# Causal attention over 1024 tokens: queries kept in natural token order, score pieces of five visits dealt anew, projections moved between visits

## The chip, the cores and the metric

The kernel runs on one NeuronCore of one Trainium2 chip. The metric is the device time of one execution in microseconds. It is given as the median of several executions. A profile is one further execution, recorded instruction by instruction.

## What is computed

`x` holds 32 images of 256 channels by 1024 tokens (32 x 32), in float32. Each image goes through a group norm (32 groups of 8 channels), a projection to queries, keys and values, causal attention with 8 heads of 32 channels in which a token sees only earlier tokens, and a residual sum. Cut to what matters, for one image:

```python
xn = _gn(x)                                     # 32 groups of 8 channels, eps 1e-5
q = einsum('oc,bcs->bos', q_w, xn) + q_b
k, v = halves of einsum('oc,bcs->bos', kv_w, xn) + kv_b
scores = einsum('bhqd,bhkd->bhqk', q, k) / sqrt(32)
scores = where(tril(ones, -1) == 0, -10000.0, scores)
attn = softmax(scores); attn = where(mask == 0, 0.0, attn)
x = x + einsum('bhqk,bhkd->bhqd', attn, v)
```

The mask leaves out the diagonal, so that the first token sees nothing.

## The kernel before, in words

**Tiling.** Channels lie on the 128 partitions in two groups `g` of four heads each. Tokens are cut into eight blocks of 128. Scores are kept transposed, keys on partitions and queries along the row, so that the exponentials can be fed to the product with the values without a transpose. No maximum is subtracted; a slow path (`shifted`) would redo everything if a sum left its range, and it isn't run here. In odd blocks the tokens of the normed input `xn` are stored backwards (`norm_apply`, L260). In the kernel before, queries, keys and values all inherit that order, and `finish` (L626) turns the result back.

**Visits.** The work of one image on one group is cut into five visits (the table `VISITS`, L676), so an image has ten, called 0 to 9 here: 0 to 4 for the first group, 5 to 9 for the second. A visit makes, for each of four heads, the scores of one key block against 512 queries ("L", tiles `sT`, one tile of two PSUM banks for each pair of heads), and against up to 384 more queries short pieces that share one tile of three banks (`tri`). ScalarE then makes three exponentials from it (L449 and L452): `e` for the first pair of heads, `e` for the second, `eh` for the short pieces. GpSimd zeroes what the mask hides (`mask`, L399). A string in `VISITS` gives the order in which TensorE gets the pieces: `2L` is the long row of head 2, `3s2` the piece "s" of head 3 in bank 2, and `W` is a wait of TensorE on its own earlier products, since two heads must not write one bank at once. The head pair that is named in the fourth entry goes into the first `sT` tile.

**The loop.** The main loop (L867) puts into each engine's queue, in this order: the scores of visit i; the first part of the products with the values of visit i-1 (`values(..., 0)`, tile `acc`); the projections that the table `PROJECT` (L765) puts at this visit; the second part of the products; the sums of keys on VectorE (`add_keys`); and what is set "after" the visit, among it the halves of the norm for the next image (`norm_apply`, placed by `PREPARE`, L766). Queues run in order, so this order is that of every engine.

**Projections.** An image has twelve units of projection: query or key, group, half of the tokens (tiles `pp`, eight units), and two token blocks of values each (tiles `ppv`, four units). Two of the ten visits take two units, the others one. `PROJECT` counts visits from the start of the image that the unit belongs to, so that -4 is visit 6 of the image before. Each unit needs a PSUM bank. `room` (L136) gives half of a tile from the pool of the `sT` tiles; that pool has two tiles in all, so they are passed round between the two pairs of heads and the projections. `lone` (L133) gives the one bank of the pool that the accumulators `acc` of the values use as well. ScalarE copies each unit out (L287, L306).

```python
ps_s = tc.alloc_tile_pool(name="ps_s", bufs=2, space=PSUM)
ps_t = tc.alloc_tile_pool(name="ps_t", bufs=1, space=PSUM)
ps_o = tc.alloc_tile_pool(name="ps_o", bufs=1, space=PSUM)
...
def lone(name):
    return ps_o.tile([P, HALF], F32, tag="acc", name=name)
```

`norm_*`, `fold`, `stack`, `sum_folded`, `invert` and `spread_inverses` make the statistics of the norm and the denominators with VectorE, GpSimd and DMAs; the change leaves them where they are.

Of the kernel before, what the change touches and what calls it, by code (L numbers as in the profile page):

```python
# [17 lines left out]
P = 128  # L18
HD = 32
# [14 lines left out]
def tile_norm_attention_residual(  # L34
# [69 lines left out]
    def unshifted():  # L104
# [68 lines left out]
        def product(out, lhsT, rhs, start=True, stop=True, more=1):  # L173


            for c in range(P // HD):
                part, n = slice(HD * c, HD * (c + 1)), more if c == 0 else 1
                width = rhs.shape[-1] // n
                for k in range(n):
                    cols = slice(k * width, (k + 1) * width)  # L180
                    nc.tensor.matmul(  # L181
                        out[part, cols], lhsT=lhsT[:, part], rhs=rhs[:, cols], start=start, stop=stop, skip_group_check=True
                    )
# [91 lines left out]
        def project_qk(b, g, n, hf, bank=room):  # L275

            key = ("qk"[n], b, g)
            if hf == 0:
                live[key] = qkpool.tile([P, S], F32, tag="qk"[n], name=f"{'qk'[n]}_{b}_{g}")
            cols = slice(hf * HALF, (hf + 1) * HALF)  # L280
            pp = bank(f"pp_{b}_{g}_{n}_{hf}")
            for cc in range(NG):
                product(
                    pp, wT[:, cc, n * C + g * P : n * C + (g + 1) * P], live["xn", b, hf][:, cc, :],
                    start=cc == 0, stop=cc == NG - 1, more=2 if (g, n, cc) == (0, 0, NG - 1) else 1,
                )
            nc.scalar.activation(  # L287
                live[key][:, cols], pp, AF.Identity, bias=qk_bias[:, n, g : g + 1], scale=(SCALE, 1.0)[n],
            )
            if (g, n, hf) == (1, 1, 0):  # L290
                nc.scalar.sem_inc(copied, 1)

        def project_v(b, n, bank=room):
# [5 lines left out]
            hf, at = divmod(2 * n * P, HALF)  # L299
            for s in range(2):  # L300
                tokens = slice(at + s * P, at + (s + 1) * P)
                for cc in range(NG):
                    product(
                        pp[:, s, :], live["xn", b, hf][:, cc, tokens], wT[:, cc, 2 * C : 3 * C], start=cc == 0, stop=cc == NG - 1,
# [3 lines left out]
        def projections(b):  # L308
# [4 lines left out]
            def v(n, *bank):  # L313
# [4 lines left out]
                qk(0, 0, 0, *early), qk(1, 0, 0), qk(0, 0, 1, *early), v(0, *early), qk(1, 0, 1), qk(0, 1, 0, lone),  # L318
                qk(1, 1, 0), v(1), v(2), v(3), qk(0, 1, 1), qk(1, 1, 1, lone),
            ]  # L320

        def both(label, kb, first, width, at=0):

            return [(label, c, at, kb, first, width) for c in (0, KEYS)]

        def row(kb, blocks, more=()):
# [3 lines left out]
                ("o", 0, 0, kb + 1, (kb + 1) * P, KEYS), ("o", KEYS, 0, kb + 1, (kb + 1) * P, P),  # L330
                ("e", 0, KEYS, kb, kb * P, blocks * P),
                ("e", KEYS, P, kb, kb * P + KEYS, blocks * P - KEYS),
            ] + list(more)

        def pieces(i):
# [4 lines left out]
            for j in range(4):  # L340
                for label, c, at, k, q, width in short:
                    at += j * SHORT
                    while width:
                        bank = at // HALF
                        n = min(width, (bank + 1) * HALF - at)
                        ops.setdefault((j, label, bank), []).append((j, c, bank, at, k, q, n))
                        at, q, width = at + n, q + n, width - n
                for label, a, b in (("L", 0, HALF), ("La", 0, HALFBANK), ("Lb", HALFBANK, HALF)):
                    ops[j, label, None] = [(j, c, None, a, kb, first + a, b - a) for c in (0, KEYS)]
            return ops  # L350

        def program(i):
# [4 lines left out]
            for word in VISITS[i][4].split():  # L357
# [3 lines left out]
                else:  # L361
                    j, label = int(word[0]), word[1:]
                    key = (j, label, None) if label[0] == "L" else (j, label[:-1], int(label[-1]))
# [19 lines left out]
        def score(b, g, to, op):  # L383

            j, c, _, at, kb, first, width = op
            rows = slice(HD * j, HD * (j + 1))
            return nc.tensor.matmul(  # L387
                to[c : c + KEYS, at : at + width], lhsT=live["k", b, g][rows, kb * P + c : kb * P + c + KEYS],
                rhs=live["q", b, g][rows, first : first + width], start=True, stop=True, skip_group_check=True,
            )  # L390

        def select(to, of, odd):

            nc.gpsimd.affine_select(  # L394
                out=to, in_=of, pattern=[[0, 4], [(1, -1)[odd], P]], compare_op=ALU.is_gt, fill=0.0, base=0,
                channel_multiplier=(-1, 1)[odd],
            )

        def mask(b, g, i):  # L399
# [3 lines left out]
            if i == 0:  # L403
                select(e[:, :, :P], e[:, :, :P], 0)
                nc.gpsimd.memset(e[0:1, :, 0:1], 1.0)
                select(eh[:, :, :P], eh[:, :, :P], 1)
            elif i < 4:
                square = epool.tile([P, 4, 2 * P], F32, tag="d", bufs=3, name=f"diagonal_{b}_{g}_{i}")
                live["e", b, g, "D", i] = square
                for s in range(2):  # L410
                    select(square[:, :, s * P : (s + 1) * P], eh[:, :, (1 - s) * KEYS : (3 - s) * KEYS], s)

        def scores(b, v):
# [6 lines left out]
            wide = max(at + width for _, _, at, _, _, width in short)  # L420
# [205 lines left out]
        def finish(b, n, within=slice(0, HALF), later=None, queue=nc.sync):  # L626
# [4 lines left out]
            start, count = within.start // P, (within.stop - within.start) // P  # L631

            def add(s):
                nc.vector.scalar_tensor_tensor(  # L634
                    blocks(rb, s), blocks(num, s, (start + s) % 2 == 1), v_bias_col[:, g : g + 1],
                    blocks(xt[:, g, cols], s), ALU.add, ALU.add,
                )

            def end():
                if cols.start == 0:  # L640
# [7 lines left out]
            parts = min(count, 2)  # L648
            return [lambda: nc.vector.tensor_mul(num, num, rb)] + [lambda s=s: add(s) for s in range(parts - 1)] + [  # L649
                lambda: (add(parts - 1), end())  # L650
            ]

        def end_last(b):
# [8 lines left out]
            for n, part in enumerate([in_range] + bounds):  # L662
# [12 lines left out]
        WHOLE = "1s0 2s1 3s2 0L 2L 1L 3L W 0s0 1s1 W 2s2"  # L675
        VISITS = [  # L676
            (0, 0, both("s", 1, P, 3 * P), (0, 2), WHOLE),
            (0, HALF, row(2, 2), (2, 3), "2e2 1e1 3La 0e0 0o0 3Lb 2L 1L 0L W 3e2 3o2 2e1 W 1o0 2o1 1e0"),
            (
                1, HALF, row(4, 1, both("x", 5, 6 * P, P + KEYS, P + KEYS)), (2, 3),  # L680
                "1e1 2x2 0x0 3Lb 0o0 1x1 2Lb 0e0 3La 1Lb 2La W 0Lb 3o2 1La 3x2 W 2o1 0La 2e1 1o0 3e2 1e0 2x1",
            ),
            (
                2, HALF, row(6, 2, both("x", 5, 7 * P + KEYS, KEYS, 2 * P + KEYS)), (0, 1),
                "3x2 1o0 2o1 0Lb 1e0 2e1 3e2 1Lb 3o2 0La 2Lb 1La 3Lb W 0o0 2La 0e0 3La 1e1 0x0 W 2e2 2x2 1x1",
            ),
            (3, HALF, both("s", 4, 5 * P, 3 * P), (0, 2), WHOLE),
# [7 lines left out]
                0, [(("H", 0, Q(0, 3)), 1, Q(1, 4)), (("H", 1, Q(1.5, 2.5)), 2, Q(3, 4))],  # L695
# [3 lines left out]
            (  # L699
                1, [(("L", 3, Q(0, 4)), 2, Q(0, 4)), (("H", 2, Q(1.5, 3)), 5, Q(2, 3.5))], [  # L700
                    (("H", 3, Q(2.5, 3)), 5, Q(3.5, 4)),
                    (("D", 2, Q(0, 1)), 4, Q(0, 1)), (("D", 2, Q(1, 2)), 5, Q(1, 2)),
                ],
            ),
# [359 lines left out]
```

## Time and profile before

| | |
|---|---|
| time, median of 3 runs | 1780.82 us (1780.32 to 1783.55) |
| time of the profiled execution | 1780.62 us |
| its span, first to last instruction | 1778.9 us |
| granted TensorE clock | 0.999 |
| busy: TensorE, VectorE, ScalarE, GpSimd | 99%, 92%, 82%, 48% |

The span divided by 32 images is 55.6 us for an image. In the timelines a row is: start and length in us, the engine (PE is TensorE, PEld its weight loads, ACT ScalarE, DVE VectorE, POOL GpSimd), the line, the operation, output tile <- input tiles, shapes, and how many of them were merged. A float32 product takes two records in the profile, so that the counts are twice those of the program. What stands in brackets is the idle time ahead of the row and what ended it.

### The profile page before, as it was taken

Reading aid. Unit: us, or ns where it says so; the run is one execution under the profiler, and the core shown is the slowest. Engines: PE = TensorE matmul, PEld = TensorE weight load, DVE = VectorE, ACT = ScalarE, POOL = GpSimd, SP = SyncE. Lnnn points to the kernel's source line nnn. Section 1 sums busy time; section 2 is a strip of 40 time slices with the busy share of each in tenths; the row PEclk is TensorE's granted clock in tenths of the full one; section 3 lists DMA queues with packets and bytes.
Section 4 is the critical chain, followed back from the end, with each engine's and each line's share of the span. In section 5 each row is a group of like instructions: output and inputs, shape, how many; then the busy total and the mean of one; then the engine's idle time right before and its main releaser. Section 6 shows DMA issues by size and latency. Waiting matters only on the chain.

```text
span 1778.9 us, 81945 instructions
## 1 busy us (share of the span) xinstructions
PE 1765.2 (99%) x37152; PEld 982.5 (55%) x37152; DVE 1631.3 (92%) x1859; ACT 1465.8 (82%) x1736; POOL 855.3 (48%) x935
## 2 busy tenths in 40 slices
PE   9999999999999999999999999999999999999997
PEld 5555555555555555555555555555555555555553
DVE  4689999999999999999999999999999999999987
ACT  6888888888888888888888888888888888888885
POOL 2445544544554455444454544555445455455541
PEclk9999999999999999999999999999999999999999
DMA  2566766766767767776677676666766676777663
GB/s 70 108 119 133 149 131 147 139 137 141 145 134 139 146 135 150 128 151 135 137 142 149 130 143 142 140 144 130 144 143 139 140 141 137 146 136 143 130 119 87
DMA packets 92772, 240.22 MB, mean 135 GB/s; under 512 B 26273, under 2 KB 27793, under 8 KB 76545
## 3 DMA queue, kind: packets, MB, share of 16 engines
q0 software_dynamic: 17360, 100.58, 38.5%
q1 hardware_dynamic: 74912, 134.28, 26.9%
q8 instruction: 291, 4.77, 1.1%
q14 instruction: 65, 0.52, 0.1%
q10 hardware_dynamic: 144, 0.07, 0.0%
HBM read 69.90 MB, written 34.95 MB: 59 GB/s over the span
## 4 chain that ended last, share of the span: by engine, by line
PE 97%; DVE 1%; DMA 1%; ACT 0%; issue 0%; SPq 0%; POOL 0%; DVEq 0%; ACTq 0%
PE acc L478 30%; PE pp L181 25%; PE tri L387 16%; PE sT L387 14%; PE ppv L181 12%; DMA rb<-inverses 0%; DMA x<-in_x_dram 0%; ACT e L449 0%; DVE rb L634 0%; DVE num L649 0%; ACT eh L452 0%; DMA inverses<-inv_turned 0%; DVE rb_last L634 0%; DVE e L497 0%; DVE st L197 0%
## 5 line engine op out<-in xcount | busy, mean ns | idle before, releaser
L449 ACT ACTIVATE e<-sT 128x1024 f32<-128x1024 f32 x640 | 620.8, 1022 | 232.5 <-PE sT L387 229.2
L387 PE MATMUL sT<-q,k 32*64 32x256 f32 (+1 forms) x7424 | 547.8, 461 | 0.3 <-issue 0.3
L387 PE MATMUL tri<-q,k 32*64 32x128 f32 (+4 forms) x12416 | 539.2, 297 | 1.0 <-ACT eh L452 0.9
L394 POOL TENSOR_SCALAR_AFFINE_SELECT diagonal<-eh 128x512 f32<-128x512 f32 x384 | 366.3, 993 | 300.3 <-ACT eh L452 300.3
L387 PEld LDWEIGHTS tri<-q,k 32*64 32x64 f32 x12416 | 387.1, 131 | 172.9 <-issue 79.9
L181 PE MATMUL pp<-xn,wT 128*32 128x512 f32 (+1 forms) x4224 | 477.6, 582 | 0.0
L497 DVE TENSOR_TENSOR e<-e,e 128x2048 f32<-128x2048 f32 x189 | 467.9, 2476 | 3.4
L497 DVE TENSOR_TENSOR e<-e,eh 128x1536 f32<-128x1536 f32 x378 | 420.7, 1113 | 41.4 <-PE acc L478 33.7
L452 ACT ACTIVATE eh<-tri 128x1536 f32<-128x1536 f32 (+1 forms) x320 | 453.4, 1417 | 1.1 <-PE pd L550 1.1
L524 POOL DMA_DIRECT2D e<-e x248 | 213.6, 861 | 368.4 <-DMA e<-e 282.4
L478 PE MATMUL acc<-e,v 128*32 128x512 f32 x2560 | 338.8, 600 | 1.5 <-POOL diagonal L394 1.5
L387 PEld LDWEIGHTS sT<-q,k 32*64 32x64 f32 x7424 | 302.8, 131 | 12.2 <-issue 0.6
L181 PEld LDWEIGHTS pp<-xn,wT 128*32 128x32 f32 x4224 | 140.6, 109 | 270.3 <-issue 215.7
L497 DVE TENSOR_TENSOR e<-e,diagonal 128x1024 f32<-128x1024 f32 x189 | 253.4, 1341 | 6.7
L181 PE MATMUL ppv<-wT,xn 128*32 128x256 f32 x4064 | 242.6, 379 | 0.0
L478 PE MATMUL acc<-eh,v 128*32 128x384 f32 (+3 forms) x3072 | 198.7, 346 | 0.0
L394 POOL TENSOR_SCALAR_AFFINE_SELECT e<-e 128x512 f32<-128x512 f32 x64 | 96.6, 1509 | 201.9 <-ACT e L449 201.9
L478 PEld LDWEIGHTS acc<-eh,v 128*32 128x32 f32 x3072 | 97.0, 110 | 143.1 <-issue 120.6
L181 PEld LDWEIGHTS ppv<-wT,xn 128*32 128x32 f32 x4064 | 130.9, 110 | 70.0 <-ACT q L287 0.3
L649 DVE TENSOR_TENSOR num<-num,rb 128x512 f32<-128x512 f32 x124 | 95.4, 790 | 62.4 <-DMA rb<-inverses 60.6
L273 ACT ACTIVATE xn<-x,shift,rstd 128x256 f32<-128x256 f32 x248 | 135.1, 593 | 0.4 <-POOL shift L258 0.4
L634 DVE SCALAR_TENSOR_TENSOR rb<-num,v_bias_col,x 128x256 f32<-128x256 f32 x248 | 123.7, 521 | 0.0
(94 smaller groups left out, 1226.9 us busy)
## 6 DMA issues: line engine op xcount, KB each, us to landing
e<-e POOLq DMA_DIRECT2D x124, 512.0 KB, 6.5
x<-in_x_dram SPq DMA_DIRECT2D x124, 256.0 KB, 4.3
e<-e POOLq DMA_DIRECT2D x124, 256.0 KB, 4.6
folded<-e SPq DMA_DIRECT2D x124, 256.0 KB, 4.5
rb<-inverses SPq DMA_DIRECT2D x124, 256.0 KB, 3.4
out_dram<-rb SPq DMA_DIRECT2D x124, 256.0 KB, 3.8
x<-in_x_dram SPq DMA_DIRECT2D x2, 512.0 KB, 3.7
inverses<-inv_turned SPq DMA_DIRECT2D x31, 32.0 KB
```

Of the source, the lines that this page charges most:

```text
L181: nc.tensor.matmul(out[part, cols], lhsT=lhsT[:, part], rhs=rhs[:, cols], start=start, stop=stop, skip_group_check=True)
L273: nc.scalar.activation(to, of, AF.Identity, bias=live["shift", b][:, g : g + 1], scale=rstd)
L387: return nc.tensor.matmul(to[c : c + KEYS, at : at + width], lhsT=live["k", b, g][rows, kb * P + c : kb * P + c + KEYS], rhs=live["q", b, ...
L394: nc.gpsimd.affine_select(out=to, in_=of, pattern=[[0, 4], [(1, -1)[odd], P]], compare_op=ALU.is_gt, fill=0.0, base=0, channel_multiplier= ...
L449: nc.scalar.activation(e[:, heads[a][0] : heads[a][1] + 1 : step, :], banks[a], AF.Exp)
L452: exp = nc.scalar.activation(eh[:, :, :wide], tri.rearrange("p (j q) -> p j q", q=SHORT)[:, :, :wide], AF.Exp)
L478: nc.tensor.matmul(acc[HD * j : HD * (j + 1), of], lhsT=live["v", b][:, kb, h * HD : (h + 1) * HD], rhs=e[:, j, :], start=first, stop=last ...
L497: nc.vector.tensor_add(to, to, tile_of(b, g, at))
L524: nc.gpsimd.dma_start(out=total[:rows], in_=total[rows : 2 * rows], accum_op=ALU.add)
L634: nc.vector.scalar_tensor_tensor(blocks(rb, s), blocks(num, s, (start + s) % 2 == 1), v_bias_col[:, g : g + 1], blocks(xt[:, g, cols], s), ...
L649: return [lambda: nc.vector.tensor_mul(num, num, rb)] + [lambda s=s: add(s) for s in range(parts - 1)] + [lambda: (add(parts - 1), end())]
```

## The change

**Queries in natural order.** The query projection reads the backward blocks of `xn` in reverse. For that, `project_qk` cuts each product of 512 columns, for queries and keys, into two of 2 x 128 (even blocks, odd blocks), and for queries the odd half is read backwards. The splitting of one product in `product` (`more`) goes. `finish` no longer turns anything back and makes one addition of 512 columns out of two of 256.

**Scores.** Visits 0 and 5 leave 64 x 64 pieces out that the mask hides, and use their place for pieces of the diagonal of block 4 ("z", in the first 64 columns of the long row; "y", among the short pieces). Visits 2 and 3 of each group share out the rest in another way: visit 3 now makes 320 short columns for each head in place of 384, visit 2 makes the 384 with fewer and longer products. The string of visit 0 becomes `2s2 0z 1s1 0y0 3L 0s0 2L 1z 1L 3z 2z 0L W ...`, and its first pair of heads is 2 and 3 in place of 0 and 2. The products with the values of visit 3 change from 512, 192 | 64, 128, 128 columns to 512, 384 | 128. A new tile `corner` holds the diagonal of block 4; `mask` fills it with two selects and a copy on GpSimd, and two selects of 128 columns become one of 128 and two of 64.

**Places of the projections.** `PROJECT` and `projections` change, and with them what shares a visit: visit 1 has two units of the second group, visit 6 two of the next image. `PREPARE` moves two operations of the norm from after visit 6 to after visit 5, and one from after visit 7 to after visit 6.

```diff
-        def product(out, lhsT, rhs, start=True, stop=True, more=1):
+        def product(out, lhsT, rhs, start=True, stop=True):
...
-            for cc in range(NG):
-                product(
-                    pp, wT[:, cc, n * C + g * P : n * C + (g + 1) * P], live["xn", b, hf][:, cc, :],
-                    start=cc == 0, stop=cc == NG - 1, more=2 if (g, n, cc) == (0, 0, NG - 1) else 1,
-                )
+            for s in range(2):
+                for cc in range(NG):
+                    product(
+                        blocks(pp, s), wT[:, cc, n * C + g * P : n * C + (g + 1) * P],
+                        blocks(live["xn", b, hf][:, cc, :], s, n == 0 and s == 1), start=cc == 0, stop=cc == NG - 1,
+                    )
...
-                qk(0, 0, 0, *early), qk(1, 0, 0), qk(0, 0, 1, *early), v(0, *early), qk(1, 0, 1), qk(0, 1, 0, lone),
-                qk(1, 1, 0), v(1), v(2), v(3), qk(0, 1, 1), qk(1, 1, 1, lone),
+                qk(0, 0, 0, *early), qk(1, 0, 0), qk(0, 0, 1, *early), qk(1, 0, 1), v(0, lone), v(1, *early),
+                qk(0, 1, 0), qk(1, 1, 0), qk(0, 1, 1, lone), v(2), qk(1, 1, 1), v(3),
...
             if i == 0:
-                select(e[:, :, :P], e[:, :, :P], 0)
+                corner = live["e", b, g, "C", i] = epool.tile([P, 4, P], F32, tag="c", bufs=1, name=f"corner_{b}_{g}")
+                select(corner[:, :, KEYS:], e[:, :, :KEYS], first=KEYS)
+                select(e[:, :, :P], e[:, :, :P])
                 nc.gpsimd.memset(e[0:1, :, 0:1], 1.0)
+                nc.gpsimd.tensor_copy(corner[:KEYS, :, KEYS:], eh[:KEYS, :, :KEYS])
+                select(eh[:, :, :P], eh[:, :, :P], 1)
...
             def end():
+                nc.vector.scalar_tensor_tensor(rb, num, v_bias_col[:, g : g + 1], xt[:, g, cols], ALU.add, ALU.add)
...
-            (0, 0, both("s", 1, P, 3 * P), (0, 2), WHOLE),
+                ], (2, 3), "2s2 0z 1s1 0y0 3L 0s0 2L 1z 1L 3z 2z 0L W 3s2 2s1 2y1 W 1s0 3y2 1y0",
...
-        PROJECT = (-5, -4, -2, -3, 0, 1, 1, -1, 2, 4, 3, 6)
-        PREPARE = (-13, -12, -10, -10, -9, -8, -7, -6, -4, -4, -3)
+        PROJECT = (-5, -4, -3, -2, -4, -1, 0, 1, 1, 2, 3, 4)
+        PREPARE = (-13, -12, -10, -10, -9, -8, -7, -6, -5, -4, -4)
...
-            for n, f in zip((None, None, 0, None, 0, 1, 1, 1) + PROJECT[8:], units):
+            for n, f in zip((None,) * 5 + (0,) + PROJECT[6:], units):
```

Three places of the queues follow, as the built programs have them. Names carry the group, the query/key number and the half: `pp_1_0_1` is the second group's query on the second half of the tokens, `e_0_1` the exponentials of visit 1. A semaphore named after an engine is a wait for that engine.

TensorE from the end of the scores of visit 1 to the first scores of visit 2, before the change. Here `pp_1_0_0` is the unit in the accumulators' bank (`lone`) and `pp_1_1_0` the one in a tile of the `sT` pool (`room`):

```order
L387 MATMUL tri_0_1_3844<-q_0_3373,k_0_3468 64x64
L181 MATMUL pp_1_0_0_3888<-xn_0_3250,wT 32x512 [waits Activation_49]
L181 MATMUL pp_1_0_0_3888<-xn_0_3250,wT 32x512 x7
L181 MATMUL pp_1_1_0_3899<-xn_0_3250,wT 32x512 [waits Activation_49]
L181 MATMUL pp_1_1_0_3899<-xn_0_3250,wT 32x512 x7
L478 MATMUL acc_0_0_3910<-e_0_0_3766,v_3572 32x512 [waits Activation_49,Pool_49]
L478 MATMUL acc_0_0_3910<-e_0_0_3766,v_3572 32x512 x3
```

The same place after the change; `pp_1_1_0` has the tile of the `sT` pool, and `pp_1_0_1` the accumulators' bank:

```order
L399 MATMUL tri_0_1_3920<-q_0_3438,k_0_3535 64x64 x2
L178 MATMUL pp_1_1_0_3966<-xn_0_3313,wT 32x2x128 [waits Activation_49]
L178 MATMUL pp_1_1_0_3966<-xn_0_3313,wT 32x2x128 x15
L178 MATMUL pp_1_0_1_3985<-xn_1_3488,wT 32x2x128 x16
L497 MATMUL acc_0_0_4003<-e_0_0_3822,v_3554 32x512 [waits Activation_49,Pool_49]
L497 MATMUL acc_0_0_4003<-e_0_0_3822,v_3554 32x512 x3
```

The two units have changed places: the one in the accumulators' bank now stands directly ahead of the accumulators, and the one in the `sT` pool directly behind the scores. In the program, its first product waits for the first exponential of visit 1, and the first product of `acc` for ScalarE's copy of the unit ahead of it. Visit 6 has the same order, with `pp_0_1_0` and then `ppv_0` of the next image.

TensorE from the last projection of visit 4 into the scores of visit 5, before:

```order
L181 MATMUL ppv_3_4158<-wT,xn_1_3494 32x256 x15
L478 MATMUL acc_0_1_4089<-eh_0_3_4034,v_3572 32x64 x4
L478 MATMUL acc_0_1_4089<-diagonal_0_2_3983,v_3572 32x128 [waits Pool_49]
L478 MATMUL acc_0_1_4089<-diagonal_0_2_3983,v_3572 32x128 x3
L478 MATMUL acc_0_1_4089<-diagonal_0_2_3983,v_3572 32x128 [waits Pool_49]
L478 MATMUL acc_0_1_4089<-diagonal_0_2_3983,v_3572 32x128 x3
L387 MATMUL tri_1_0_4200<-q_1_3887,k_1_3898 64x128 [waits Activation_49]
L387 MATMUL tri_1_0_4200<-q_1_3887,k_1_3898 64x128
L387 MATMUL tri_1_0_4200<-q_1_3887,k_1_3898 64x256 x2
L387 MATMUL tri_1_0_4200<-q_1_3887,k_1_3898 64x384 x2
L387 MATMUL sT_1_0_0_4198<-q_1_3887,k_1_3898 64x512 x4
L387 MATMUL sT_1_0_1_4199<-q_1_3887,k_1_3898 64x512 [waits Activation_49]
```

And after:

```order
L178 MATMUL ppv_3_4223<-wT,xn_1_3488 32x256 x15
L497 MATMUL acc_0_1_4147<-corner_0_3860,v_3554 32x128 x4
L399 MATMUL tri_1_0_4256<-q_1_3876,k_1_3965 64x128 [waits Activation_49]
L399 MATMUL tri_1_0_4256<-q_1_3876,k_1_3965 64x128
L399 MATMUL sT_1_0_1_4255<-q_1_3876,k_1_3965 64x64
L399 MATMUL tri_1_0_4256<-q_1_3876,k_1_3965 64x256 x2
L399 MATMUL tri_1_0_4256<-q_1_3876,k_1_3965 64x64
L399 MATMUL sT_1_0_0_4254<-q_1_3876,k_1_3965 64x512 [waits Activation_49]
```

The products with the values behind the projection shrink from three groups of four to one, and the second `sT` tile to be written (in both programs that is the one that waits for ScalarE's copy of `ppv_3`) now comes behind a 64-column piece of the other tile, in place of the four long rows of a whole pair of heads. Visit 9 and visit 0 of the next image have the same two rows of waits.

ScalarE from the copy of visit 5's projection to the first exponential of visit 6, before and then after:

```order
L287 ACTIVATE q_0_5968<-pp_0_0_0_5969,qk_bias 128x512 [waits PE_49,Activation_49]
L487 COPY num_0_1_5999<-acc_0_1_5819 128x512 [waits PE_49]
L449 ACTIVATE e_1_1_6011<-sT_1_1_0_6013 128x1024 [waits DMASW6_49,DMAHW6_49,DMASW5_49,PE_49]
L449 ACTIVATE e_1_1_6011<-sT_1_1_1_6014 128x1024 [waits PE_49]
L452 ACTIVATE eh_1_1_6012<-tri_1_1_6015 128x4x320 [waits DVE_49,PE_49,Pool_49]
```

```order
L285 ACTIVATE q_0_6039<-pp_0_0_0_6040,qk_bias 128x512 [waits PE_49,Activation_49]
L506 COPY num_0_1_6077<-acc_0_1_5881 128x512 [waits PE_49]
L270 ACTIVATE xn_1_6089<-x_5192,shift_5800,rstd_5695 128x2x128 [waits DMAHW7_49]
L270 ACTIVATE xn_1_6089<-x_5192,shift_5800,rstd_5695 128x2x128
L468 ACTIVATE e_1_1_6092<-sT_1_1_0_6094 128x1024 [waits DMASW6_49,DMAHW6_49,DMASW5_49,PE_49]
```

Two operations of the norm have moved in ahead of the first exponential of visit 6.

More of the change, by code (lines that the diff above doesn't have):

```diff
@@ L171, in keep_busy @@
                 nc.tensor.matmul(pt[:width, 0, :width], lhsT=ident[:, :width], rhs=ident[:, :width], start=True, stop=True)
-        def product(out, lhsT, rhs, start=True, stop=True, more=1):
+        def product(out, lhsT, rhs, start=True, stop=True):
             for c in range(P // HD):
[L177 to L182, printed above, removed]
-                    )
+                part = slice(HD * c, HD * (c + 1))
+                nc.tensor.matmul(
+                    out[part], lhsT=lhsT[:, part], rhs=rhs, start=start, stop=stop, skip_group_check=True
+                )
         def blocks(tokens, s, turned=False):
@@ L646, in end @@
                     later(send)
[L648 to L651, printed above, removed]
+            return [lambda: nc.vector.tensor_mul(num, num, rb), end]
         def end_last(b):
```

125 lines of the change are left out of this document (66 added, 59 removed).

## The prediction

> **What bounds the kernel now.** I read the page first, then the waits of TensorE, then a table by stretches, and then the timelines of TensorE and ScalarE over a few visits.
>
> ```profile
> span 1778.9 us, 81945 instructions
> PE 1765.2 (99%) x37152; PEld 982.5 (55%) x37152; DVE 1631.3 (92%) x1859; ACT 1465.8 (82%) x1736; POOL 855.3 (48%) x935
> PE 97%; DVE 1%; DMA 1%; ACT 0%; issue 0%; SPq 0%; POOL 0%; DVEq 0%; ACTq 0%
> PE acc L478 <- POOL diagonal L394: 1.5, 1, 1.5
> PE pp L181 <- ACT k L287: 0.8, 1, 0.8
> 900.00:955.40 55.40, 55.40 (x1164) 30.56 (x1160) 52.21 (x60) 46.62 (x56) 27.88 (x31) 1.00 0.72 142
> ```
>
> The chain that ends last is TensorE's for 97% of the span. Its two longest waits add up to 2.3 us of 1778.9, and over one image of 55.4 us it has no idle time at all. So TensorE's work and its waits set the time: what its stages lose or gain counts in full, and every new wait counts in full. VectorE (52.2 us of 55.4), ScalarE (46.6) and GpSimd (27.9) have room.
>
> The changed order matters in three places of each group of five visits. The profiled execution took 1780.62 us, within 0.2 us of the median 1780.82, so I add to it and leave the difference.
>
> **Wait (a), the projection behind the scores of visits 1 and 6.** The timelines of TensorE and ScalarE around a visit 1, the group of the exponentials, and the one place of the start where TensorE waits for a copy:
>
> ```profile
> 897.69 0.39 PE L387 MATMUL tri<-q,k 32*64 32x64 f32 x4
> 899.28 3.64 PE L181 MATMUL pp<-xn,wT 128*32 128x512 f32 x32
> 902.74 1.04 PE L478 MATMUL acc<-e,v 128*32 128x512 f32 x8
> 898.93 1.94 ACT L449 ACTIVATE e<-sT 128x1024 f32<-128x1024 f32 x2 [0.52 <-PE sT L387]
> 902.99 0.69 ACT L287 ACTIVATE k<-pp,qk_bias 128x512 f32<-128x512 f32 x1 [0.42 <-PE pp L181]
> L449 ACT ACTIVATE e<-sT 128x1024 f32<-128x1024 f32 x640 | 620.8, 1022 | 232.5 <-PE sT L387 229.2
> 24.56 2.76 PE L181 MATMUL pp<-xn,wT 128*32 128x512 f32 x24
> 27.38 0.69 ACT L287 ACTIVATE k<-pp,qk_bias 128x512 f32<-128x512 f32 x1 [0.79 <-PE pp L181]
> 28.12 1.93 PE L181 MATMUL pp<-wT,xn 128*32 128x256 f32 x32 [0.81 <-ACT k L287]
> ```
>
> Scores start at 897.69, the two units of projection at 899.28. The first exponential runs from 898.93 for 1.02 (row L449), to 899.95. Today the unit in the accumulators' bank goes first and needs none of it. After the change the unit in the `sT` pool goes first, and its tile is the one that this exponential reads. From the end of ScalarE's row at 28.07 to TensorE at 28.12 it took 0.05, so the unit can start at 900.00: 0.72 us of wait where there was none, at visit 1 of 32 images. Visit 6 has two operations of the norm ahead of its exponential in addition:
>
> ```profile
> 870.58 0.58 ACT L487 COPY num<-acc 128x512 f32<-128x512 f32 x1
> 871.69 1.94 ACT L449 ACTIVATE e<-sT 128x1024 f32<-128x1024 f32 x2 [0.53 <-PE sT L387]
> 913.79 1.08 ACT L273 ACTIVATE xn<-x,shift,rstd 128x256 f32<-128x256 f32 x2
> ```
>
> ScalarE was idle 0.53 us at that place, and two such operations take 1.08, so the exponential comes about 0.45 later, allowing 0.1 for the overlap of ScalarE's rows: 1.17 us at visit 6 of 31 images. Sum (a): 0.72 x 32 + 1.17 x 31 = 59.3 us.
>
> **Wait (b), the accumulators behind the projection in their own bank.** The rows at 24.56 to 28.12 above show this case once today: a projection ends at 27.32, ScalarE copies it from 27.38 to 28.07, and TensorE goes on at 28.12, idle 0.81. In the steady state today, another unit of 1.73 us lies between. After the change `acc` follows the unit directly, twice in an image. Without a wait it would start before the unit's last product ends:
>
> ```profile
> 906.34 1.91 PE L181 MATMUL ppv<-wT,xn 128*32 128x256 f32 x32
> 908.07 0.62 PE L478 MATMUL acc<-diagonal,v 128*32 128x128 f32 x16
> 911.24 1.90 PE L181 MATMUL pp<-xn,wT 128*32 128x512 f32 x16
> 912.96 1.04 PE L478 MATMUL acc<-e,v 128*32 128x512 f32 x8
> L306 ACT COPY v<-ppv 128x512 f32<-128x512 f32 x127 | 74.4, 586 | 2.4 <-PE ppv L181 1.0
> ```
>
> The next work starts 1.73 after the start of a unit that ends after 1.91, so 0.18 more is lost: 0.99 us behind a query (visit 1), and 0.88 behind values, whose copy takes 0.59 in place of 0.69 (visit 6). Sum (b): 0.99 x 32 + 0.88 x 31 = 59.0 us. Behind TensorE's waiting product stand only its own scores of the next visit; ScalarE waits for those, and has no other work that could be drawn forward.
>
> **Wait (c), the long rows of visits 0 and 5.** The second `sT` tile that is written waits for ScalarE's copy of the values projected before:
>
> ```profile
> 915.62 1.06 PE L478 MATMUL acc<-e,v 128*32 128x512 f32 x8
> 916.82 1.91 PE L181 MATMUL ppv<-wT,xn 128*32 128x256 f32 x32
> 918.55 0.29 PE L478 MATMUL acc<-eh,v 128*32 128x64 f32 x8
> 918.66 0.62 PE L478 MATMUL acc<-diagonal,v 128*32 128x128 f32 x16
> 919.21 0.56 PE L387 MATMUL tri<-q,k 32*64 32x128 f32 x6
> 919.25 0.64 PE L387 MATMUL sT<-q,k 32*64 32x512 f32 x2
> 920.90 1.06 PE L478 MATMUL acc<-e,v 128*32 128x512 f32 x8
> 922.43 1.92 PE L181 MATMUL pp<-xn,wT 128*32 128x512 f32 x18
> 917.32 1.46 ACT L452 ACTIVATE eh<-tri 128x1536 f32<-128x1536 f32 x1
> 918.80 0.58 ACT L306 COPY v<-ppv 128x512 f32<-128x512 f32 x1
> ```
>
> Today the copy is over at 919.38, and the scores start at 919.21; four long rows lie ahead of the first one that needs the tile. After the change the products ahead of the projection are 512 and 384 columns, as in the rows from 920.90 to 922.43: 1.53 in place of 1.20. The projection then starts at 917.15 and ends at 919.06; the copy lasts until 919.71, and TensorE can go on at 919.76. The products behind the projection shrink from 0.66 (918.55 to 919.21) to some 0.33 (half of the 0.55 from 918.66, and the tail), so the scores still start at 919.21. But `3L` now comes after some seven short pieces (0.05 us to issue, as six records take 0.04 to the row at 919.25), and stands from 919.26 to 919.76. Everything behind it stands too, and head 3 has nothing before it, so the stage becomes longer by the whole 0.50. Sum (c): 0.50 x 63 = 31.5 us.
>
> **What is gained.** Lengths of the scores, from their first row to the next work: visit 1 1.59 (897.69 to 899.28), visit 5 1.69 (919.21 to 920.90), and visit 3:
>
> ```profile
> 908.62 0.35 PE L387 MATMUL tri<-q,k 32*64 32x64 f32 x6
> 910.36 1.06 PE L478 MATMUL acc<-e,v 128*32 128x512 f32 x8
> ```
>
> That is 1.74, and visit 2 has the same pieces. Visit 3 becomes like visit 1 (320 short columns, much the same pieces): -0.15. Visit 2 keeps its 384 columns in 24 products in place of 43; visit 5 needs 1.69 for them in 20: about 1.70, -0.04. Visit 0 goes from 20 to 28: +0.01. Together -0.18 x 64 = -11.5 us. The products with the values keep their sum (1.53 + 0.33 against 1.20 + 0.66). Query and key units become as finely cut as the value units: 1.73 against 1.72 above, 256 units, +2.5 us. In visits 3 and 8 the second `sT` tile is reached sooner; its copy ends some 0.3 to 0.4 into the scores, about where it is wanted: 0 to 7 us, I take 3.
>
> At nothing I cost: the merged addition in `finish` and the merged sums (VectorE, below its limit); the shorter exponential of visit 3 (ScalarE, below it); GpSimd's two or three more operations for a group, which have at least the scores of the next visit as cover (without it, a wait like the 1.5 us of `acc` on `diagonal` in the waits above); the moved units' copies on ScalarE, since each visit keeps its number of units; the start and the end of the program, 2 us either way.
>
> [...]
>
> **Sum.** 59.3 + 59.0 + 31.5 - 11.5 + 2.5 + 3 = 143.8. 1780.6 + 143.8 = 1924 us.
>
> **The rivals.**
>
> 1. The waits stay hidden and the kernel gets faster. For: two units in one visit cost no wait today, and less is computed. Against: that rests on the order of the two units, which has been turned round. The time would be 1780.6 - 11.5 + 2.5 = 1771.6. It decides at 0.14 us of wait for each of the 63 groups; (b) alone is some 0.9. Chance 4%, and 1% for something within 0.2% of the time before, about what measurement of this kernel can tell.
>
> 2. Only the accumulators' wait shows in full. The order of visit 1 starts head 3 early, so that the first exponential may come sooner, and 3L may find its tile copied. (a) can't go under 0.4 us: a long row of 512 columns takes at least 0.85 (half of the 1.73 in which a unit streams 1024 such columns), and 0.85 + 1.02 + 0.1 is past 1.59. Time: 1780.6 + 0.4 x 63 + 59.0 - 9 = 1856. Chance 8%.
>
> 3. Reading backwards is slow on TensorE. No row shows it. On ScalarE odd blocks are read backwards today at no visible cost:
>
> ```profile
> L273 ACT ACTIVATE xn<-x,shift,rstd 128x256 f32<-128x256 f32 x248 | 135.1, 593 | 0.4 <-POOL shift L258 0.4
> 882.03 0.61 ACT L273 ACTIVATE xn<-x,shift,rstd 128x256 f32<-128x256 f32 x1
> ```
>
> The single one is a backward half, 0.61 against a mean of 0.59 over both kinds. If TensorE took twice as long, half of four query units of 1.73 would add 3.46 us to an image: 1924 + 111 = 2035. Below nothing isn't to be had, since the columns are the same. Chance 5%.
>
> 4. The pauses lower the clock. If the stage behind each of the four long pauses of an image (a projection of 1.73, products of 0.97) ran at half speed, it would add 2 x (1.73 + 0.97) x 31.5 = 170: 2094. Chance 2%.
>
> The forecast itself has the remaining 80%. Its own range: (a) moves by 0.25 us a time (16), (b) by 0.1 (6), (c) between 0.2 and 0.7 (-19, +13), the scores by 5, start and end by 2; about 1880 to 1965. To leave out no more than 2 in 10 it reaches down to rival 2: 1856 to 1965. Slower 0.95, faster 0.04, same 0.01.
>
> **What would show it.** In the changed profile TensorE's waits should list `pp` on ScalarE's `e` 63 times with some 0.7 to 1.2 us, `acc` on ScalarE's `q` and `v` copies 63 times with about 0.8 and 0.7 us of idle time, and `sT` on `v` 63 times with about 0.5. TensorE's busy share should fall to 93 to 95%, and scores of visit 3 should take 1.6 us. The forecast is wrong if an image's stretch shows TensorE without idle time, if query units take longer than key units, or if the granted clock falls below 1.00.

## The result, and the profile after

The changed kernel takes 1962.91 us (median of 4 runs, 1958.14 to 1966.85); before it was 1781.18 beside them. The ratio is 1.1017 (95% interval 1.099 to 1.1044): slower, by more than the 1924 forecast, and close under the upper end of the range. The profiled execution took 1963.14 us. First its page, and its chain of waits:

```profile
span 1961.4 us, 82054 instructions
PE 1831.6 (93%) x37144; PEld 1089.5 (56%) x37144; DVE 1579.3 (81%) x1668; ACT 1458.8 (74%) x1736; POOL 959.0 (49%) x1191
q8 instruction: 291, 4.77, 1.0%
PE 86%; ACT 8%; issue 3%; DMA 2%; DVE 1%; POOL 1%; ACTq 0%; SPq 0%; DVEq 0%; POOLq 0%
```

TensorE was busy for 99% and is now for 93%. ScalarE, which had no part of the chain, has 8% of it. The third line is used further down; "issue" in the last one, 3%, is time in which TensorE waited for nothing that the profile shows. TensorE's waits (total us, times, longest):

```profile
PE pp L178 <- ACT e L468: 57.2, 63, 1.1
PE acc L497 <- ACT q L285: 28.8, 32, 0.9
PE acc L497 <- ACT v L304: 24.7, 31, 0.8
PE tri L399 <- issue: 4.6, 8, 1.1
PE sT L399 <- issue: 1.4, 1, 1.4
```

The first three are waits (a) and (b), at 63 places each, as named. The last two were not foreseen. The sign that was named for (c), `sT` on `v` in this list, isn't in it: other products of TensorE are still running at that place. The list of the weight loads has it, at 62 places:

```profile
PEld sT L399 <- ACT v L304: 20.9, 62, 0.3
```

A visit 1 on TensorE, and below it on ScalarE:

```profile
1531.87 0.28 PE L399 MATMUL tri<-q,k 32*64 32x64 f32 x4
1534.43 3.66 PE L178 MATMUL pp<-xn,wT 128*32 128x256 f32 x64 [0.91 <-ACT e L468]
1538.99 1.07 PE L497 MATMUL acc<-e,v 128*32 128x512 f32 x8 [0.90 <-ACT q L285]
```

```profile
1533.36 1.94 ACT L468 ACTIVATE e<-sT 128x1024 f32<-128x1024 f32 x2 [0.77 <-PE sT L399]
1538.16 0.69 ACT L285 ACTIVATE q<-pp,qk_bias 128x512 f32<-128x512 f32 x1 [1.04 <-PE pp L178]
```

The first exponential starts 1.49 us after the scores, not 1.24, and the projection waits for it. The two units then stream 64 products, a query and a key unit alike, and `acc` stands until ScalarE has copied the second one. Visit 6 is the same with the norm's operations ahead of the exponential. In visit 0 the rows of TensorE show wait (c) as a hole between two groups of scores, and ScalarE's row shows what fills it:

```profile
1525.63 0.33 PE L399 MATMUL tri<-q,k 32*64 32x128 f32 x2
1525.77 0.53 PE L399 MATMUL tri<-q,k 32*64 32x64 f32 x5
1526.18 0.64 PE L399 MATMUL sT<-q,k 32*64 32x512 f32 x2
```

```profile
1525.55 0.59 ACT L304 COPY v<-ppv 128x512 f32<-128x512 f32 x1 [0.34 <-PE ppv L178]
```

The long row starts 0.04 behind the end of the copy (1526.14). The stages, as the mean of 27 images each, the fourth to the thirtieth (us; from the first row of a visit's scores to that of the next visit; the third column is an experiment told below):

| visit | before | changed | changed, without GpSimd's transfers |
|---|---|---|---|
| 0 | 5.70 | 6.24 | 6.24 |
| 1 | 6.02 | 8.36 | 8.12 |
| 2 | 4.90 | 4.86 | 4.86 |
| 3 | 5.31 | 5.67 | 5.29 |
| 4 | 5.29 | 5.28 | 5.28 |
| 5 | 5.73 | 6.24 | 6.24 |
| 6 | 6.03 | 8.17 | 8.13 |
| 7 | 4.90 | 4.86 | 4.86 |
| 8 | 5.34 | 5.39 | 5.40 |
| 9 | 5.29 | 5.28 | 5.28 |
| image | 54.50 | 60.34 | 59.68 |

**The stops.** In visits 1 and 3 the length varies from image to image, which no wait of the theory explains: visit 3's scores take 1.59 us in the best images and 3.72 in the worst. A visit without such a stop is called undisturbed below. One such visit 3, on TensorE:

```profile
943.51 1.15 PE L399 MATMUL sT<-q,k 32*64 32x256 f32 x11
946.03 0.58 PE L399 MATMUL sT<-q,k 32*64 32x512 f32 x1 [1.37 <-issue]
946.03 0.76 PE L399 MATMUL tri<-q,k 32*64 32x64 f32 x20
```

TensorE and its weight loads stand together. A record is an entry of the profile for a product, a weight load or one of about 80 other instructions of TensorE's queue, most of them for semaphores. Counting these from the start, gaps of 0.5 to 2.0 us in visit 3 lie behind records 22208, 29120, 31424, 33728 and 36032: each is a multiple of 256, plus 192. The page has 37144 + 37144 products and weight loads of TensorE and 291 packets of instructions, one for 255 records. And in the window from 943.6 to 944.6 us the DMA view shows one of them:

```profile
q8 instruction: 1, 0.02, 5.8%
```

TensorE goes on 1.4 us behind that packet. What stood ahead of it in the queues, on GpSimd and SyncE:

```profile
936.95 0.89 POOL L543 DMA_DIRECT2D e<-e  x1
```

```profile
937.80 5.61 SPq L655 DMA_DIRECT2D out_dram<-rb  x3
```

The first is one of GpSimd's accumulating transfers (two for each sum of the keys, 512 and 256 KB), the second the results on their way out. TensorE passed the beginning of the block before at 938.8, and the packet began only at 943.65.

### The profile page after: what moved, and what is told of

Read it like the earlier page. It is cut to its first block, busy times and chain, and to the rows that moved or that the text cites. A ratio compares the mean times of both kernels' runs of the same rounds, so it can differ in the third digit from the quotient of the medians.

```text
span 1961.4 us, 82054 instructions
## 1 busy us (share of the span) xinstructions
PE 1831.6 (93%) x37144; PEld 1089.5 (56%) x37144; DVE 1579.3 (81%) x1668; ACT 1458.8 (74%) x1736; POOL 959.0 (49%) x1191
## 3 DMA queue, kind: packets, MB, share of 16 engines
q8 instruction: 291, 4.77, 1.0%
## 4 chain that ended last, share of the span: by engine, by line
PE 86%; ACT 8%; issue 3%; DMA 2%; DVE 1%; POOL 1%; ACTq 0%; SPq 0%; DVEq 0%; POOLq 0%
PE acc L497 26%; PE pp L178 23%; PE tri L399 13%; PE sT L399 12%; PE ppv L178 11%; ACT e L468 3%; ACT q L285 2%; ACT xn L270 2%; ACT v L304 1%; DVE e L516 1%; DMA e<-e 1%; PE pd L569 0%; DMA out_dram<-rb 0%; DMA wn<-in_L_conv_kv_w_dram 0%; POOL diagonal L406 0%
## 5 line engine op out<-in xcount | busy, mean ns | idle before, releaser
L399 PE MATMUL tri<-q,k 32*64 32x64 f32 (+5 forms) x10752 | 573.1, 315 | 7.4 <-issue 4.6
L399 PE MATMUL sT<-q,k 32*64 32x512 f32 (+3 forms) x6144 | 563.7, 527 | 1.6 <-issue 1.4
L178 PE MATMUL pp<-xn,wT 128*32 128x256 f32 x8192 | 485.8, 380 | 57.4 <-ACT e L468 57.2
L178 PEld LDWEIGHTS pp<-xn,wT 128*32 128x32 f32 x8192 | 253.9, 110 | 280.1 <-ACT e L468 113.5
L406 POOL TENSOR_SCALAR_AFFINE_SELECT diagonal<-eh 128x256 f32<-128x256 f32 (+1 forms) x384 | 345.1, 997 | 109.5 <-ACT eh L471 96.5
L399 PEld LDWEIGHTS sT<-q,k 32*64 32x64 f32 x6144 | 260.6, 131 | 32.9 <-ACT v L304 20.9
L497 PE MATMUL acc<-eh,v 128*32 128x384 f32 (+1 forms) x2560 | 200.3, 404 | 0.0
L516 DVE TENSOR_TENSOR e<-e,diagonal 128x1024 f32<-128x1024 f32 x126 | 156.0, 1238 | 6.7
L406 POOL TENSOR_SCALAR_AFFINE_SELECT corner<-eh 128x256 f32<-128x256 f32 x64 | 37.6, 588 | 224.1 <-ACT eh L471 224.1
L285 ACT ACTIVATE q<-pp,qk_bias 128x512 f32<-128x512 f32 x128 | 88.0, 688 | 74.1 <-PE pp L178 74.1
```

The source lines that it names most:

```text
L178: nc.tensor.matmul(out[part], lhsT=lhsT[:, part], rhs=rhs, start=start, stop=stop, skip_group_check=True)
L285: nc.scalar.activation(live[key][:, cols], pp, AF.Identity, bias=qk_bias[:, n, g : g + 1], scale=(SCALE, 1.0)[n],)
L399: return nc.tensor.matmul(to, lhsT=live["k", b, g][rows, kb * P + c : kb * P + c + KEYS], rhs=of, start=True, stop=True, skip_group_check=True
L406: nc.gpsimd.affine_select(out=to, in_=of, pattern=[[0, 4], [1, to.shape[-1]]], compare_op=ALU.is_gt, fill=0.0, base=first - (P - 1 if odd ...
L497: nc.tensor.matmul(acc[HD * j : HD * (j + 1), of], lhsT=live["v", b][:, kb, h * HD : (h + 1) * HD], rhs=e[:, j, :], start=first, stop=last ...
L516: nc.vector.tensor_add(to, to, tile_of(b, g, at))
```

## The experiments

**1. The lone unit first again.** The two units of visits 1 and 6 change places in the changed kernel; nothing else is undone.

```diff
-                qk(0, 1, 0), qk(1, 1, 0), qk(0, 1, 1, lone), v(2), qk(1, 1, 1), v(3),
+                qk(0, 1, 0), qk(0, 1, 1, lone), qk(1, 1, 0), v(2), qk(1, 1, 1), v(3),
...
-                    for n, f in zip(PROJECT, projections(b)):
+                    units = list(zip(PROJECT, projections(b)))
+                    for n, f in units[:1] + units[4:5] + units[1:4] + units[5:]:
                         when(first + n, f)
```

> The changed kernel with one thing undone: in visits 1 and 6 the unit in the accumulators' bank is projected ahead of the unit in the sT pool again; everything else stays changed. Theory (the order of the two units makes waits (a) and (b)): the wait of pp on the exponential goes (2566 - 1588 = 0.98 us at visit 1, 2675 - 1588 = 1.09 at visit 6 by the changed kernel's trace), and of the wait of acc (1.11 and 1.03) all but some 0.25 us goes: the long exponential of the short tile ends 4.56 us after the scores' start, the lone unit's copy another 0.69 later, and acc would start at 1.59 + 3.46 = 5.05. That is (0.98 + 0.86) x 32 + (1.09 + 0.80) x 31 = 118 us less: 1963 - 118 = 1845, and down to 1825 if the irregular stops in visits 1 and 3 go too. Rival (the order of the units is not what costs; reading backwards, the finer cut or the new pieces are): less than 30 us less, 1933 or more.

Measured: 1841.39 us, ratio to before 1.0322 (1.0304 to 1.034). TensorE's waits begin with

```profile
PE tri L399 <- ACT eh L471: 2.6, 2, 2.0
PE busy L171 <- POOL ident masks.py:199: 1.7, 1, 1.7
PE tri L399 <- issue: 1.6, 3, 1.0
```

and the 63 waits of `pp` and the 63 of `acc` are gone from it. So 121.5 us of the 182 are the order of two units, and the rival is out. Visits 1 and 6 without a stop take 6.27 and 6.28 (6.02 and 6.03 before): the 0.25 are the expected lateness of the copy that `acc` waits for.

**2. The same order alone, in the kernel before.**

```diff
-                qk(0, 0, 0, *early), qk(1, 0, 0), qk(0, 0, 1, *early), v(0, *early), qk(1, 0, 1), qk(0, 1, 0, lone),
-                qk(1, 1, 0), v(1), v(2), v(3), qk(0, 1, 1), qk(1, 1, 1, lone),
+                qk(0, 0, 0, *early), qk(1, 0, 0), qk(0, 0, 1, *early), v(0, *early), qk(1, 0, 1), qk(1, 1, 0),
+                qk(0, 1, 0, lone), v(1), v(2), v(3), qk(0, 1, 1), qk(1, 1, 1, lone),
...
-                        when(first + n, f)
+                        at.setdefault(first + n, []).insert(0 if n == -4 else len(at.get(first + n, ())), f)
```

> The kernel before with one thing of the change alone: in visits 1 and 6 the unit in the sT pool is projected ahead of the unit in the accumulators' bank. Theory by the prediction's terms: (a) 0.72 us at each of 63 places (no operation of the norm stands ahead of visit 6's exponential here) and (b) 0.99: (0.72 + 0.99) x 63 = 108 us more, 1781 + 108 = 1889; with (b) as the changed kernel shows it (1.11) 1896. A second theory on the size of (a): the changed kernel's 0.98 at visit 1 comes from its own string of scores, which puts the second half of head 3's long row behind head 1's; here it should be 0.72 then. If it is 0.98 here too, the string is not the reason, and the time is about 1912. Rival (the order costs nothing by itself): 1781.

Measured: 1966.11 us, ratio 1.1006 (1.0978 to 1.1035). Its waits:

```profile
PE pp L181 <- ACT e L449: 40.5, 63, 0.7
PE acc L478 <- ACT q L287: 27.9, 31, 0.9
PE acc L478 <- ACT k L287: 27.9, 31, 0.9
PE tri L387 <- issue: 27.9, 20, 3.8
PE acc L478 <- issue: 11.8, 8, 3.5
```

Scores and wait of an undisturbed visit 1 or 6 take 2.315, so (a) is 2.315 - 1.588 = 0.73, the forecast's 0.72 (40.5 / 63 = 0.64 of it shows as idle time). So the 0.98 of the changed kernel is its own string of scores. (b) is 1.08. That makes 114 us; the other 70 were expected by none of the theories. They are stops again, in visits 2, 3, 7 and 8, up to 3.8 us long, and the half clock that follows the longest (last section). In the scores of visits 3 and 8 those over 0.3 us stand behind a record that is 192 above a multiple of 256. Five visits 1 are 0.5 to 0.9 us longer at another record. In these five GpSimd issues its gather for the norm (`eight`, L216) 0.3 to 0.7 us after the scores' start, in the other 22 at 1.0 or later; whether that is the cause wasn't tested.

**3. The beginnings of the blocks moved.** 32 more products in the warm-up, 128 records.

```diff
-            keep_busy(56, HD)
+            keep_busy(88, HD)
```

> The changed kernel with 32 products more in the warm-up ahead of the norm (128 records of TensorE more, some 3 us). Nothing else is moved. Theory on the irregular stops (TensorE waits for nothing that the profile shows, in visits 1 and 3): it waits for its own instructions, which come in blocks of 256 records by packets of 16 KB, and the stop stands where a block begins. Then the block begins 128 records earlier in every visit: no stop is left at the old records (visit 1 within 0.2 to 0.8 us of the scores' start, visit 3 at 1.07), the mean of visit 1's scores and wait falls from 2.81 towards 2.57 and visit 3's scores from 2.02 to 1.59: 20 us less, 3 us more at the start, 1946, unless the new places of the beginnings fall behind late packets too; new stops, if any, stand 128 records earlier. Rival (the stops come from transfers or from GpSimd that use the same memory at that time, or from a wait that the profile doesn't show): they stay at the same places in visits 1 and 3, 1966.

Measured: 1995.78 us, ratio 1.1191 (1.1169 to 1.1213). Visits 1 and 3 have no stop in any of the 27 images (2.566 and 1.588 us in every one), which only the theory of the blocks says. But the time grew: the beginnings of the blocks now lie in the scores of visit 6, where two loads of a later image are issued, and there the mean of scores and wait went from 2.69 to 3.89 us. That of the two units went from 4.49 to 4.98, with half the clock behind some of the stops (last section). That it is the loads that hold the packet up there was not shown apart. One such visit on TensorE, and the DMA view of 845.2 to 846.3 us:

```profile
847.72 1.14 PE L399 MATMUL sT<-q,k 32*64 32x512 f32 x6 [1.70 <-issue]
```

```profile
q8 instruction: 1, 0.02, 5.6%
```

Where the stops stand is shown; the 1946 for the time failed, because the new places are worse.

**4. The piece 0z later**, in visits 0 and 5.

```diff
-"2s2 0z 1s1 0y0 3L 0s0 2L 1z 1L 3z 2z 0L W ..."
+"2s2 1s1 0y0 3L 0s0 2L 0z 1z 1L 3z 2z 0L W ..."
```

> The changed kernel with one piece moved: in visits 0 and 5 the small piece 0z, the first one that touches an sT tile, stands behind 2L, so that 3L's tile is the first that is touched. Theory of term (c): the first tile touched finds a free buffer and the second waits for the copy of the values; with 3L first, the scores of visits 0 and 5 go from 2.22 us back to about 1.69: 0.53 x 63 = 33 us less, 1963 - 33 = 1930. Rival (the 0.53 us is the price of the new pieces, 28 products in place of 20, or 3L waits for that copy whichever tile it has): 1963.

Measured: 1936.28 us, ratio 1.0852 (1.0835 to 1.0868), 27 us less. The scores of visits 0 and 5 take 1.80, not 1.69: the wait was 0.42 of the 0.53 (26.5 us over 63 visits), and the line of the weight loads that wait for `v`, 62 times, is gone from their list. The other 0.11 I put to the new pieces (28 products for 20), which no run takes away. Both readings are right in part, and the theory in the larger. In the profiled execution the gain was 22 us, as visit 1's stops cost 0.2 us more there. The `W` of the strings stood in every run, so that what it guards against is not shown.

**5. Without GpSimd's accumulating transfers**, in the changed kernel and, as run 6, in the kernel of run 2. One line is left out of both:

```diff
-            nc.gpsimd.dma_start(out=total[:rows], in_=total[rows : 2 * rows], accum_op=ALU.add)
```

> The changed kernel without GpSimd's accumulating transfers (two for each of four sums of an image, 512 and 256 KB); so the sums of the keys lack three quarters of their rows, and everything else is as in the changed kernel. Theory (the packet that brings TensorE's next block of instructions waits behind these transfers): all irregular stops of visits 1 and 3 go; visit 1's scores and wait have a mean of 2.57 us in place of 2.81, visit 3's scores 1.59 in place of 2.02, visits 0, 2 and 4 to 9 stay; 20 us less, 1943. Second theory (the rows sent out and the spread of the inverses, SyncE's transfers, hold the packet up as well): stops remain in visit 3, where three transfers to the output stand, and the gain is about 10 us. Rival (the packets are not what TensorE stops for): stops as before, 1963.

Measured: 1943.04 us, ratio 1.0905 (1.0888 to 1.0921), the 1943 expected. TensorE's waits have no stop left among the first:

```profile
PE pp L178 <- ACT e L468: 60.7, 63, 1.0
PE acc L497 <- ACT q L285: 28.8, 32, 0.9
PE acc L497 <- ACT v L304: 24.7, 31, 0.8
PE tri L399 <- ACT eh L471: 2.6, 2, 2.0
```

and all ten visits have their undisturbed lengths (the table's last column). The transfers out of visit 3 alone, which are still there, stop nothing: visit 3 takes 5.29 us.

**6. The same line left out, in the kernel of run 2.**

> The kernel before with the two units of visits 1 and 6 in the other order, and without GpSimd's accumulating transfers (the sums of the keys lack three quarters of their rows). With the transfers this order took 1966 us, of which the waits (a) and (b) as its trace has them are (0.73 + 1.08) x 63 = 114; the other 70 us are stops in visits 1, 3, 7 and 8 at the first record of a block of TensorE's instructions. Theory (the packet with the block waits behind the accumulating transfers): the stops go, and the time is 1781 + 114 = 1895 to 1900. Second theory (SyncE's transfers hold it up as well): between 1905 and 1945. Rival: 1966.

Measured: 1913.87 us, ratio 1.0745 (1.0728 to 1.0761). 52 of the 70 us are gone. In the scores, stops remain in 15 of 27 visits 8 and nowhere else. SyncE's transfers `rb<-inverses` are issued there, from 1.7 us ahead of the beginning of the block before to that beginning, which fits the second theory. But they are issued at the 12 visits 8 without a stop too, and leaving them out was not tried, so that what holds the packet up there stays open.

**7. The half row earlier** in the scores of visits 1 and 6.

```diff
-"1o1 2o2 3La 0o0 1e1 0e0 2L 1L 3Lb 0L W ..."
+"1o1 2o2 3La 0o0 1e1 0e0 2L 3Lb 1L 0L W ..."
```

> The changed kernel with the second half of head 3's long row one place earlier in the scores of visits 1 and 6, ahead of head 1's long row. Theory on the size of (a) (the first exponential waits for that half row): at visit 1 it starts 1.24 us after the scores' start in place of 1.49, and the projection 0.25 sooner where no stop disturbs it; at visit 6 the operations of the norm end 1.6 us after the start in any case, so nothing changes there. 0.25 x 32 = 8 us less, 1955. Rival (it starts late because the short pieces take longer to issue): 1963 with the exponential at 1.49.

Measured: 1952.87 us, ratio 1.095 (1.0933 to 1.0967). The first exponential on ScalarE of an undisturbed visit 1, whose scores start at 1528.83:

```profile
1530.11 1.94 ACT L468 ACTIVATE e<-sT 128x1024 f32<-128x1024 f32 x2 [0.56 <-PE sT L399]
```

That is 1.28 after the start in place of 1.49, and the wait fell by 0.20, to 0.78. The 10 us hold 6 from this. The other 4 are not accounted for: visit 1's stops moved, but cost as much as before (scores and wait 2.64 in the mean, 2.36 undisturbed).

**8. All waits undone** (runs 1, 4 and 7 together, and one number of the norm's plan):

```diff
-        PREPARE = (-13, -12, -10, -10, -9, -8, -7, -6, -5, -4, -4)
+        PREPARE = (-13, -12, -10, -10, -9, -8, -7, -6, -6, -4, -4)
```

> The changed kernel with all of its waits undone: the unit in the accumulators' bank first in visits 1 and 6, the piece 0z later in visits 0 and 5, the half row of visits 1 and 6 earlier, and two operations of the norm a visit earlier, so that none is ahead of visit 6's exponential. If the waits (a), (b) and (c) are all that the change costs beside the stops, the stages sum to 5.82 + 6.03 + 4.86 + 5.29 + 5.28 + 5.82 + 6.03 + 4.86 + 5.40 + 5.28 = 54.67 us for an image, 0.17 more than before: 1781 + 5 = 1786, and with stops as in the run with the lone unit first (13 us at visit 1, 2 at visit 3) 1800. The change itself would then bring nothing: its gain in scores, some 0.18 us an image, is used up by the pieces of visits 0 and 5 and by the query units. If a cost has been overlooked: 1815 or more.

Measured: 1812.27 us, ratio 1.0171 (1.0157 to 1.0185). Stages of an image: 55.62 in the mean, and 54.84 if of each visit the shortest is taken. Visits 1 and 6 are 6.07 and 6.04 then, the two waits gone; in the mean they are 6.53 and 6.34, so that irregular lengths cost 0.76 us an image, 24 us. The plan of the norm cost 0.14 in visit 5, where four of its operations now stand ahead of the exponential. The expectation of 1786 to 1800 was too low, and what lies above 1786 is these two: 24 us, and 0.14 at 31 visits 5, some 4. No version here beats the kernel before, and none is in sight: even undisturbed, 54.84 is over 54.50.

## Why the prediction was right, and where it was too small

The mechanisms were the forecast's: 63 waits of (a), 63 of (b), and (c) in visits 0 and 5. (a) and (b) were shown together by taking them away (run 1) and by adding them alone (run 2), part of (a) by itself in run 7, and (c) in run 4. Its sizes, undisturbed lengths times the counts:

| term | forecast | measured |
|---|---|---|
| (a) visit 1, visit 6 | 0.72, 1.17: 59.3 | 0.98, 1.09: 65.1 |
| (b) visit 1, visit 6 | 0.99, 0.88: 59.0 | 1.11, 1.00: 66.5 |
| (c) | 0.50: 31.5 | 0.42: 26.5 |
| scores, with the pieces of visits 0 and 5 | -0.18: -11.5 | -0.15 - 0.05 + 0.11: -5.5 |
| the rest (halves of pp, second sT tile of visits 3 and 8) | 5.5 | 10 (what is left of 163) |
| stops for instructions | none | 20 |

Sum: 143.8, against 163 without the stops and 184 with them (5.18 and 5.84 us an image by the table of stages, for some 31.5 images); the medians differ by 182. That 1963 still lies inside the range, 2 us under its end, is in part luck: about half of the 39 us that the forecast lacks are stops, and the range had no share for these.

- **(a) at visit 1** was taken from the row of the old scores, where the first exponential starts 1.24 after them. The new string puts `3Lb` behind `1L`, and the exponential follows it to 1.49. The prediction quoted no row for the new order; run 7 gives 0.20 of the 0.26 back, and run 2 with the old string has the 0.73.
- **(b)** took an idle time of 0.81 from the start of the program, where two units had followed each other. In the steady state it is 0.90 behind a query: TensorE went on 0.05 us after the copy at the start of the program, and takes 0.14 here (1538.85 to 1538.99 in the rows above). Why `acc` takes longer stays open.
- **(c)** was right in kind; I put the whole difference down to the copy, and made the pieces free (+0.01), where 0.11 is left for them.
- **The rest:** the second `sT` tile of visits 3 and 8 was left at 3 us. The products behind those scores took 0.10 longer in both visits, and the scores of visit 8 stayed at 1.68 in place of 1.59. No run shows that the second tile is the reason.
- **The step that was missing** is the stops. I costed start and end, and every wait by semaphore, and took for granted that TensorE's instructions are there. The profile of the kernel before has a single clear one, in visit 3 of the third image, which is 0.76 us longer. In the table's images its scores of visits 3 and 8 have none: there, where a block of 256 records lasts only some 4.4 and 3.9 us, the packet starts 0.3 to 1.9 us after the beginning of the block before. In the changed kernel the beginnings meet other transfers, and in visit 3 it starts up to 4.9 us after that beginning.

**The rivals.** Rival 1 and rival 2 are out by the waits. Reading backwards costs nothing that shows: a query unit streams 1.727 us, as key units do, and rival 3 is out. On rival 4: the forecast charged the pauses nothing beyond their length. The start of the kernel before has one of 0.81 us, with the granted clock in the column after GpSimd's:

```profile
26.00:30.00 4.00, 3.19 (x52) 1.32 (x44) 0.00 (x0) 1.28 (x3) 1.22 (x2) 1.00 0.00 0
```

Half speed, which rival 4 supposes, is in no row of the prediction; the runs show it behind longer stops (last section). The changed profile has a granted clock of 0.999 in the mean, and the window of the stop above reads

```profile
943.00:947.00 4.00, 2.63 (x68) 1.46 (x68) 1.33 (x2) 2.15 (x4) 3.49 (x5) 1.00 0.25 91
```

Four pauses of 0.8 to 1.1 us in each image, and a stop of 1.37, left it at 1.00. A longer wait near the end of the program, 1.95 us for `eh`, has 3.4 us of half clock behind it. Rival 4 is out.

## What to carry to other kernels

Where two units share a stage, ask of each what it needs first and who needs its buffer next: the order alone was worth 6% here, and 121 of 182 us. Take a wait's size from the new order's rows, not from the old order's. And TensorE's instructions come by transfers too, 291 packets here: with GpSimd's accumulating transfers left out the changed kernel lost its stops, 20 us (run 5). So ask what is issued just ahead of the beginning of a block.

## What the runs showed of the hardware

**TensorE's instructions came in blocks of 256 records**, 16 KB a packet (4.77 MB in 291). Over the ten profiles TensorE has 105 idle times of more than 0.15 us for which no releaser shows, and 104 of them stand where a block begins. The places move with 128 more records ahead (run 3), and the ten stops of the changed kernel end 1.2 to 1.6 us after the packet's end. Without GpSimd's accumulating transfers it has none. In the changed kernel 77% of the packets start behind the beginning of the block before their own, by up to 4.9 us, and the others at most 1.1 us ahead of it.

**Half the clock followed most long stops.** In run 2, a stop of 3.4 us and what followed, on TensorE and in the windows (us, busy times, then the granted clock):

```profile
929.04 0.48 PE L387 MATMUL tri<-q,k 32*64 32x64 f32 x7 [3.39 <-issue]
929.45 1.94 PE L478 MATMUL acc<-e,v 128*32 128x512 f32 x8
931.16 3.58 PE L181 MATMUL pp<-xn,wT 128*32 128x512 f32 x18
```

```profile
925.30:929.40 4.10, 0.71 (x29) 0.48 (x14) 0.00 (x0) 1.86 (x2) 0.79 (x1) 0.80 0.56 120
929.40:931.20 1.80, 1.80 (x19) 0.44 (x16) 0.00 (x0) 1.45 (x1) 0.09 (x1) 0.50 1.34 137
931.20:934.60 3.40, 3.40 (x26) 1.11 (x22) 3.09 (x3) 0.00 (x0) 2.64 (x3) 0.51 0.24 53
934.60:936.00 1.40, 1.40 (x28) 0.56 (x28) 1.40 (x3) 0.69 (x1) 0.00 (x0) 1.00 1.10 176
```

The products with the values took 1.71 us in place of 0.88, and the projection 3.41 in place of 1.72. Of that run's pauses, all eight of 2.1 us and more were followed by a clock of 0.50, and none of 1.5 and less. These runs show no sharp limit between: in run 3 pauses of 1.5 to 2.1 us had it too, and one of 2.3 had not.
